# Single steps of a planned order checked by their own engines, second gate and yt tiles, and a last image in two halves

## The chip, the cores and the metric

The kernel runs on one core of a Trainium2 chip. The metric is the device time of one execution in microseconds. One further execution was taken with the hardware profiler; its trace is what the views below come from.

## The reference

Four layers on a batch of 4 images of 96 channels by 64x64 pixels (4096 tokens each), all in 32-bit floats. `gn` and `ln` are group norm and layer norm without weights.

```
x = x + ssm(gn(x))      # layer 0: 3x3 depthwise conv, 4 directional selective scans over 4096 tokens, 192 channels x 16 states
x = x + dcn(gn(x))      # layer 1: deformable 3x3 conv: offsets and mask by conv, bilinear gather of 9 taps
t = tokens(x)
t = t + fft_mix(ln(t))  # layer 2: 96->192, relu, FFT over tokens, relu of a diagonal complex map, inverse FFT, 192->96
t = t + qffn2(ln(t))    #          96->384->96, inputs and weights rounded to 8 bits (5 exponent, 2 mantissa), sums to 16
t = t + linattn(ln(t))  # layer 3: (q k^T) v for 6 heads without softmax
t = t + qffn3(ln(t))    #          as qffn2
```

The scan step is `h = exp(d*A)*h + d*u*B`, `y = C.h`, with `d = softplus(...)`. The linear attention has no softmax, so `k^T v` (96x96) is summed over all tokens first and then multiplied by `q`. A sum over the tokens is thus needed before any token's result.

## The kernel before

The program is written out by a planner on the host. Work is cut into steps: a Python generator issues some instructions and yields `cost(pe=..., dve=..., act=..., pool=...)`, its estimated time on TensorE (PE), VectorE (DVE), ScalarE (ACT) and GpSimd (POOL), or `wait(us)` for a DMA. `Clock` keeps an estimated end for each engine. The order in which the steps are drawn is the order in which each engine gets its instructions, and `in_program_order` keeps it so; each engine works through its own list in that order.

The scan is the frame. `Layer0.scan` walks over 1536 units (4 images x 4 directions x 4 stretches of 1024 tokens x 24 groups of 8 channels by 16 states). A unit is: an ACT exponential of `da` (L1003), a PE spread into `db` (L1009), a DVE multiply (`enter`, L1023), a DVE scan (`recur`, L1031), a POOL multiply (`weigh`, L1040) and PE sums into `py` (L1059). After each unit `clock.due` rises by `PACE` = 4.5 us, and two streams may fill what room is left:

- `ends`: `l0.first()` for image 0 (convolution and softplus), weights of layers 2 and 3, `l0.before(b)` for images 1 to 3 (convolution, then softplus), and then layers 2 and 3 of images 0 to 3 one after the other (`Layers23.image`). Each image waits until layer 1 has sampled it.
- `middle`: for each image `l0.behind(b)` (merge of the directions, after its scans) and `l1.image(b)` (offsets, positions, and 288 gathers, L1372, with their sums).

Where the scan can't go on, or has ended, `alone()` moves an own clock in steps of 0.5 us and offers it to the streams.

`pipe` runs several generators ("chains") of one kind side by side. It draws a chain's next step only if each engine that this step used when it last ran (`known`) is not too far ahead of the clock (`AHEAD`: 3, 3, 5, 7 us), if its tile tokens are free, and if it keeps `every` steps behind the chain before. Steps outside a `pipe`, here called single steps (group norm statistics, reciprocal roots, positions, waits for loads), are checked by `Stream.step`:

```
        if not self.piped and not (net.has_bank() and net.clock.has_room((1.0,) * 4, self.ready)):
            return False
```

So a single step needs room on all four engines, whichever it uses.

The parts that the change touches:

- `steps` (L812) makes the softplus, 48 chains an image. `ex`, `lw` and `w1` are 128x512 tiles. ACT writes `lw` (L834) and `w1` (L835), DVE combines `w1` (L838), POOL subtracts into `lw` (L840), DVE makes `rl` (L842) and frees `lw`. The pipes give `ex=3, lw=1, rl=2, du=2`.
- `Fourier.half` ends with `last` (L1573), eight chains a half: eight small products into PSUM (`yp`, L1579), an ACT copy into `yt` (L1581), one product with the weights (`o`, L1584), a DVE add to `t` (L1586). There is one `yt`.
- `centred` (L462) makes a layer norm's centred values chunk by chunk (512 tokens), gathers the variances of eight chunks in rows of one PSUM bank, and takes the reciprocal root for all at once; `normed` (L1592) spreads it again (L515) and multiplies (L1603).
- `Ffn.run` (L1633) and `LinearAttention.run` (L1699) work on all 4096 tokens: the norm first, then eight chunks of 512 (for keys and values 32 blocks of 128).
- After the scan five PSUM banks belong to the first stream and three to the other (`mm`, `has_bank`).

Of the kernel before, what the change touches and what calls it, by code (L numbers as in the profile page):

```python
# [8 lines left out]
F32 = mybir.dt.float32  # L9
# [312 lines left out]


class Stream:


    def __init__(self, net, work):
        self.net, self.work, self.ready, self.over, self.piped = net, work, 0.0, False, False
        self.held = 0

    def step(self):

        net = self.net
        net.stream = self
        if self.over or self.ready > net.clock.now():
            return False
        if not self.piped and not (net.has_bank() and net.clock.has_room((1.0,) * 4, self.ready)):
            return False
        step = next(self.work, False)
        if step is False:  # L340
            self.over = True
            return False
        self.piped = step is None or step is BLOCKED
        if isinstance(step, Step):
            self.ready = net.clock.queue(step, net.clock.now())
        return step is not BLOCKED


class Net:
# [38 lines left out]
    def mm(self, name, p=128):  # L388
        own = self.own_banks and self.stream is self.streams[0]
        return (self.own_banks if own else self.psum).tile([128, CH], F32, name=name, tag="mm")[:p]  # L390

    def has_bank(self):
        if self.own_banks:
            return self.stream.held < (5 if self.stream is self.streams[0] else 3)
        return sum(stream.held for stream in self.streams) < 3
# [65 lines left out]

    def centred(self, x, cen, dst, key, pool, bias=None):  # L462


        nc = self.nc
        var = self.mm(f"lnv{key}")
        self.hold(1)
        sqs = {}

        def chain(j):  # L470
            yield wait(new=True, takes="sq")
            cs = slice(j * CH, (j + 1) * CH)
            pc = self.mm(f"lnc{key}_{j}")
            nc.tensor.matmul(pc, lhsT=cen, rhs=x[:, cs], start=True, stop=True)  # L474
            pc = pc[:C]
            sq = sqs[j] = pool.tile([C, CH], F32, name=f"lnq{key}_{j}", tag="lnq", bufs=4)
            d, view = dst(j)
            if bias is None:
                nc.scalar.activation(sq, pc, AF.Square)
                nc.scalar.copy(d, view(pc))  # L480
            else:
                nc.scalar.activation(sq, pc, AF.Square, bias=bias)
                nc.scalar.activation(d, view(pc), AF.Identity, bias=bias)
            yield cost(pe=1.1, act=1.2, frees=f"v{j // 4}")

        def sums(r):

            yield wait(takes=f"v{r}")
            for q in range(4):
                nc.tensor.matmul(  # L490
                    var[32 * q : 32 * q + 32],
                    lhsT=self.to_row[C][:C, 1 - r : 33 - r],
                    rhs=sqs[4 * r + q],
                    start=(r == 0),
                    stop=(r == 1),
                )
            yield cost(pe=1.3, frees="sq sq sq sq")

        def chains():
            for r in range(2):  # L500
                for q in range(4):
                    yield chain(4 * r + q)
                yield sums(r)

        yield from pipe(self, chains(), 5, every=-99, sq=4, v0=-3, v1=-3)
        self.rstd = pool.tile([128, CH], F32, name=f"lns{key}", tag="lns", bufs=1)
        nw = pool.tile([128, CH], F32, name=f"lnw{key}", tag="lnw", bufs=1)
        yield from self.inv_sqrt_steps(self.rstd, var, nw, 128)
        self.hold(-1)

    def spread(self, rstd, j, n, key):
# [31 lines left out]
class Layer0:  # L543
# [54 lines left out]
    def first(self):  # L598
# [5 lines left out]
        with tc.tile_pool(name=f"l0u{b}", bufs=1) as up, tc.tile_pool(name=f"l0b{b}", bufs=1) as sm:  # L604
# [5 lines left out]
            with tc.tile_pool(name=f"l0a{b}", bufs=1) as big, tc.tile_pool(name=f"l0i{b}", bufs=1) as cp:  # L610
# [4 lines left out]
                def rows_first():  # L615
# [10 lines left out]
                    net, rows_first(), 6, every=2, lane=Layer0.conv.__code__,  # L626
                    ex=3, lw=1, rl=2, du=2, zt=1, **tokens,
                )
# [6 lines left out]

            yield from pipe(net, columns(), 5, every=2, ex=3, lw=1, rl=2, du=2)

    def before(self, b):
        net = self.net
        tc, nc, ins = net.tc, net.nc, net.ins  # L640
        with tc.tile_pool(name=f"l0u{b}", bufs=1) as up:
# [3 lines left out]
            with tc.tile_pool(name=f"l0b{b}", bufs=1) as sm:  # L645
# [12 lines left out]

                yield from pipe(self.net, chains(), 5, every=2, ex=3, lw=1, rl=2, du=2)

# [32 lines left out]
    def normed_rows(self, b, x, pad):  # L693
# [3 lines left out]
        with tc.tile_pool(name=f"l0n{b}", bufs=2) as sm:  # L697
# [17 lines left out]

            yield from net.centred(x, cen, lambda j: (rows(pad, j), as_rows), f"0_{b}", sm, bias)
            rs = net.rstd

# [93 lines left out]
    def steps(self, b, ks, j, us, dtw, sm, xdbl):  # L812
# [19 lines left out]
        nc.scalar.activation(ex, ex, AF.Exp, scale=-1.0)  # L832
        lw, w1 = tile_of("lw", 1), tile_of("w1", 1)
        nc.scalar.activation(lw, ex, AF.Ln, bias=net.one)  # L834
# [600 lines left out]
class Fourier:  # L1435
# [6 lines left out]
    def __init__(self, ctx, net):  # L1442
# [16 lines left out]
        nc.sync.dma_start(self.w2[:C], ins["w2"])  # L1459
        self.yt = wp.tile([C + 1, 8, 64], F32, name="yt")  # L1460

# [65 lines left out]
    def half(self, key, g, tv, t, pool, big):  # L1527
# [45 lines left out]
        def last(m):  # L1573
# [4 lines left out]
            for q in range(8):  # L1578
                nc.tensor.matmul(pt[:, q, :], lhsT=d[:, m + q, :], rhs=m2[:, q, :], start=True, stop=True)  # L1579
            yt = self.yt  # L1580
            nc.scalar.copy(yt[:C], pt)  # L1581
# [6 lines left out]

        yield from pipe(self.net, (last(m) for m in range(0, 64, 8)), 4, yt=1)


def normed(net, t, tl, key, pool):  # L1592

    yield from net.centred(
        t, net.cen96, lambda j: (tl[:C, j * CH : (j + 1) * CH], plain), key, pool
    )
    rs = net.rstd

    def chain(j):
        cs = slice(j * CH, (j + 1) * CH)  # L1600
        pb = net.spread(rs, 32 * (j % 4) + j // 4, C, key)
        yield cost(pe=1.2, holds=1)
        net.nc.vector.tensor_mul(tl[:C, cs], tl[:C, cs], pb)  # L1603
        yield cost(dve=0.7)

    yield from pipe(net, (chain(j) for j in range(NCH)), 3)


class Ffn:
# [22 lines left out]

    def run(self, b, t):  # L1633
        net, n = self.net, self.n
        tc, nc = net.tc, net.nc
        with tc.tile_pool(name=f"fb{n}_{b}", bufs=1) as big, tc.tile_pool(name=f"fs{n}_{b}", bufs=2) as pool:
            tl = big.tile([C, L], F32, name=f"fl{n}_{b}", tag="tl")
            yield from normed(net, t, tl, f"f{n}_{b}", pool)

# [46 lines left out]

            yield from pipe(self.net, (chunk(j) for j in range(NCH)), 4, xq=2, h16=2, h8=2, o16=2)


class LinearAttention:  # L1690
# [7 lines left out]

    def run(self, b, t):  # L1699
        net = self.net  # L1700
        tc, nc = net.tc, net.nc
        with tc.tile_pool(name=f"l3b{b}", bufs=1) as big, tc.tile_pool(name=f"l3s{b}", bufs=2) as pool:
            tl = big.tile([C + 1, L], F32, name=f"tl3{b}", tag="tl")
            nc.gpsimd.memset(tl[C:], 1.0)
            yield from normed(net, t, tl, f"3_{b}", pool)
            net.hold(1)
            pa = net.mm(f"pa{b}", C)[:, :C]

            def keys_and_values(m):
# [4 lines left out]
                yield cost(pe=0.55, act=0.4)  # L1714
                nc.tensor.matmul(pa, lhsT=kv[:, 1, :], rhs=kv[:, 0, :], start=(m == 0), stop=(m == 31))
                yield cost(pe=0.4)

            yield from pipe(self.net, (keys_and_values(m) for m in range(32)), 3)

            vk = pool.tile([C, C], F32, name=f"vk{b}", tag="vk")  # L1720
            nc.vector.tensor_mul(vk, pa, self.heads)
            net.hold(-1)
            yield cost(dve=0.3)
            p1 = net.mm(f"p1{b}", C)[:, :128]
            nc.tensor.matmul(p1, lhsT=vk, rhs=self.wff, start=True, stop=True)
            m1 = pool.tile([C, 128], F32, name=f"m1{b}", tag="m1")
            nc.scalar.copy(m1, p1)
            yield cost(pe=0.6, act=0.3)
            p2 = net.mm(f"p2{b}", C + 1)[:, :128]
            nc.tensor.matmul(p2, lhsT=self.wqT, rhs=m1, start=True, stop=True)  # L1730
            m2 = pool.tile([C + 1, 128], F32, name=f"m2{b}", tag="m2")
            nc.scalar.copy(m2, p2)
            yield cost(pe=0.6, act=0.3)

# [7 lines left out]

            yield from pipe(self.net, (chunk(j) for j in range(NCH)), 3)


class Layers23:
# [12 lines left out]
    def image(self, b):  # L1759
        net = self.net  # L1760
        while b not in self.net.sampled:
            yield BLOCKED
        with net.tc.tile_pool(name=f"t{b}", bufs=1) as tp:
            t = tp.tile([C, L], F32, name=f"t{b}", tag="t")
            net.nc.sync.dma_start(t, self.x2[b])
            yield wait(4.0)
            yield from self.fourier.run(b, t)
            yield from self.ffn2.run(b, t)
            yield from self.attn.run(b, t)
            yield from self.ffn3.run(b, t)  # L1770
            yield NOTHING
            net.nc.sync.dma_start(self.out[b], t)

# [9 lines left out]
def layers23(net, x2, out):  # L1783
# [4 lines left out]
    with ExitStack() as ctx:  # L1788
# [20 lines left out]

        streams = net.streams = [Stream(net, ends()), Stream(net, middle())]  # L1810
        clock = net.clock
# [53 lines left out]
```

## Time and profile before

| | us |
|---|---|
| median of 3 runs | 8710.01 |
| lowest, highest | 8709.18, 8720.84 |
| the profiled execution, its own time | 8725.68 |
| span of its trace | 8723.9 |
| first scan, end of the last scan | 190, 7515 |
| image 3's `t` load begins | 8261 |
| image 3's first layer norm of FFN 2 | 8541 |

All times inside the trace count from the start of its span. The busy table lists, for a stretch of the span, each engine's busy time and the number of its instructions, then the mean clock that TensorE was granted (1 is full), the share of the DMA engines and the bytes moved. The chain of waits lists start, length and engine of each piece of the work that ended last. The timeline lists start, length, engine, line and tiles, and in brackets the idle time before it with what ended it.

### The profile page before, as it was taken

To read this page: it belongs to the slowest core of one execution; us is meant where nothing else is said; L and a number is where in the kernel's file an instruction comes from. 1 tells how busy PE (TensorE), PEld (TensorE's weight loads), DVE (VectorE), ACT (ScalarE), POOL (GpSimd) and SP (SyncE) were. 2 spreads that over 40 slices of the span, in tenths; PEclk is the share of its full clock that TensorE was granted. 3 is DMA by queue.
4 is the path that set the end of the run, shared out by engine and by line. 5 is a ranking of instruction groups with operands and counts; after the bars stand their busy time and mean duration, and the time that the engine had idled before them with its cause. 6 is when DMAs were issued, how large, how long until landed. Compare 5 with 4: busy or idle time off the path is not lost.

```text
span 8723.9 us, 97214 instructions
## 1 busy us (share of the span) xinstructions
PE 6608.9 (76%) x31960; PEld 2859.5 (33%) x31960; DVE 6836.1 (78%) x5155; ACT 4925.0 (56%) x9030; POOL 5608.7 (64%) x4291
## 2 busy tenths in 40 slices
PE   6675777759767777887676788777778887789697
PEld 2211221112222332321222245422335541267383
DVE  2799889978799898778799888788988888547514
ACT  5554566636467776555577666454766665322323
POOL 0465566656579898656588887565888877347200
PEclk9765787769667777886687788776778887788788
DMA  3677678877789999766799988866879997355110
GB/s 94 160 206 186 167 199 218 211 169 193 181 217 242 242 239 231 177 169 178 194 244 239 236 222 215 188 173 165 215 207 233 229 224 170 90 153 172 56 54 13
DMA packets 773820, 1608.33 MB, mean 184 GB/s; under 512 B 264065, under 2 KB 355741, under 8 KB 771206
## 3 DMA queue, kind: packets, MB, share of 16 engines
q10 hardware_dynamic: 244224, 843.17, 38.3%
q1 hardware_dynamic: 455366, 532.37, 23.7%
q0 software_dynamic: 73728, 226.57, 9.8%
q8 instruction: 257, 4.21, 0.2%
q14 instruction: 245, 2.01, 0.1%
HBM read 1345.43 MB, written 256.29 MB: 184 GB/s over the span
## 4 chain that ended last, share of the span: by engine, by line
PE 25%; DVE 15%; DMA 7%; ACT 5%; issue 4%; SPq 1%; POOL 1%; ACTq 1%; DVEq 0%; POOLq 0%
DVE hh L1031 7%; DVE db L1023 4%; PE f L1499 3%; PE ps L1405 3%; PE py L1059 3%; PE pd L1421 2%; DMA da<-de 2%; ACT g L1384 1%; PE db L1009 1%; PE pc L752 1%; PE h L1540 1%; PE yp L1579 1%; DMA m<-in_dft 1%; ACT da L1003 1%; PE lnc L474 1%
## 5 line engine op out<-in xcount | busy, mean ns | idle before, releaser
L1040 POOL TENSOR_TENSOR hh<-hh,bc 128x1024 f32<-128x1024 f32 x1536 | 3661.0, 2386 | 377.2 <-DVE hh L1031 274.3
L1031 DVE TENSOR_TENSOR_SCAN hh<-da,st,db 128x1024 f32<-128x1024 f32 x1152 | 2700.6, 2344 | 189.4 <-PE py L1059 74.0
L1023 DVE TENSOR_TENSOR db<-db,bc 128x1024 f32<-128x1024 f32 x1536 | 1864.0, 1214 | 604.4 <-PE db L1009 602.7
L1003 ACT ACTIVATE da<-da,w_al 128x1024 f32<-128x1024 f32 x1536 | 1737.5, 1145 | 511.8 <-DMA da<-de 168.1
L1372 POOL DMA_INDIRECT g<-table,idx x1152 | 1212.7, 1053 | 373.8 <-issue 173.6
L1009 PE MATMUL db<-du,rep 24*128 24x512 bf16 x3072 | 710.0, 461 | 858.3 <-DVE hh L1031 803.5
L1059 PE MATMUL py<-hh,w_fold 128*32 128x512 f32 x6144 | 1107.7, 796 | 16.2 <-issue 11.5
L1384 ACT ACTIVATE g<-g,wt 128x96 f32<-128x96 f32 x3456 | 963.6, 364 | 136.9 <-PE py L1059 34.3
L1031 DVE TENSOR_TENSOR_SCAN hh<-da,db 128x1024 f32<-128x1024 f32 x384 | 877.3, 2285 | 84.6 <-PE py L1059 40.7
L1405 PE MATMUL ps<-w_ident,g 128*96 128x128 f32 x3744 | 736.1, 342 | 176.3 <-ACT g L1384 101.2
L1009 PEld LDWEIGHTS <-rep 24*128 24x128 bf16 x3072 | 159.6, 94 | 1963.0 <-issue 1289.7
L1038 POOL COPY st<-hh 128x1 f32<-128x1 f32 x1152 | 235.0, 204 | 741.5 <-DVE hh L1031 688.6
L1405 PEld LDWEIGHTS ps<-w_ident,g 128*96 128x96 f32 x3744 | 511.3, 149 | 548.6 <-ACT g L1384 239.0
L840 POOL TENSOR_TENSOR lw<-lw,w 128x512 f32<-128x512 f32 x192 | 243.9, 1270 | 683.7 <-DVE w L838 649.0
L752 PE MATMUL pc<-pad,wc 96*128 96x512 f32 x1152 | 579.6, 643 | 32.7 <-DMA wc<-wc_d 23.3
L871 PE MATMUL pr<-ex,w_ident 128*128 128x512 f32 x384 | 305.7, 889 | 174.7 <-DVE ex L861 81.9
L1413 ACT COPY st<-ps 96x384 f32<-96x384 f32 x384 | 178.8, 472 | 422.0 <-PE ps L1405 385.5
L752 PEld LDWEIGHTS pc<-pad,wc 96*128 96x128 f32 x1152 | 221.0, 202 | 361.5 <-issue 314.3
L829 PE MATMUL pd<-xd,w_dtw 103*64 103x512 f32 (+1 forms) x512 | 275.7, 821 | 52.7 <-DVE rl L842 18.8
L1421 PE MATMUL pd<-st,wdc 96*128 96x256 f32 x1152 | 308.9, 419 | 1.3 <-DVE d L1548 1.1
L1508 ACT COPY d<-f 128x512 f32<-128x512 f32 x192 | 111.9, 583 | 301.8 <-PE f L1499 297.1
L1059 PEld LDWEIGHTS py<-hh,w_fold 128*32 128x32 f32 x6144 | 158.5, 125 | 355.2 <-issue 282.9
(252 smaller groups left out, 8915.4 us busy)
## 6 DMA issues: line engine op xcount, KB each, us to landing
da<-de ACTq DMA_DIRECT2D x1536, 512.0 KB
du<-du SPq DMA_DIRECT2D x1536, 96.0 KB
bc<-bcd SPq DMA_DIRECT2D x128, 512.0 KB
y<-yb SPq DMA_DIRECT2D x384, 128.0 KB
de<-rl SPq DMA_DIRECT2D x128, 256.0 KB
m<-in_dft SPq DMA_DIRECT2D x128, 256.0 KB
ad<-y ACTq DMA_DIRECT2D x192, 128.0 KB
table<-pix SPq DMA_DIRECT2D x256, 96.0 KB
```

The costliest lines, as they stand in the source:

```text
L752: nc.tensor.matmul(pp, lhsT=wc[:, q, g * 128 : (g + 1) * 128], rhs=pad[:, r0 + dy : r0 + dy + NR, dx : dx + W], start=(q == 0), stop=(q == 8),
L871: nc.tensor.matmul(pr, lhsT=net.ident, rhs=ex, start=True, stop=False)
L1003: self.net.nc.scalar.activation(u.da, u.da, AF.Exp, scale=self.al[:, a : a + 1])
L1009: self.net.nc.tensor.matmul(db[:, h, :], lhsT=self.rep[64 * u.q + 32 * h : 64 * u.q + 32 * h + 24], rhs=u.du[64 * u.q + 32 * h : 64 * u.q ...
L1023: self.net.nc.vector.tensor_mul(u.db, u.db, u.bc[:, 0, :])
L1031: nc.vector.tensor_tensor_scan(u.along(u.hh), u.along(u.da), u.along(u.db), first, ALU.mult, ALU.add)
L1040: self.net.nc.gpsimd.tensor_mul(u.hh, u.hh, u.bc[:, 1, :])
L1059: nc.tensor.matmul(py[p0 : p0 + 32], lhsT=self.fold[:, u.i, :], rhs=hc[:, h * CH : (h + 1) * CH], start=u.sums["add"] is None and u.i == 0 ...
L1372: nc.gpsimd.indirect_dma_start(out=g[:, k, :], out_offset=None, in_=self.tables[b % 2], in_offset=bass.IndirectOffsetOnAxis(ap=idx[:, n : ...
L1384: nc.scalar.activation(pixel, pixel, AF.Identity, scale=wt[:, n, c : c + 1])
L1405: nc.tensor.matmul(pt[:, k, :], lhsT=g[:, k, c * C : (c + 1) * C], rhs=net.ident, is_transpose=True, start=(c == 0), stop=(c == corners - 1),)
L1421: nc.tensor.matmul(po, lhsT=wdc[:, k, :], rhs=st[:, k, :], start=(k == 0), stop=(k == 8))
```

## The change

A single step is now checked by the work it had when the program last stood at the same place (code object and line of the innermost generator); only at an unknown place are all four engines asked for room.

```
+def place(steps):
+    while steps.gi_yieldfrom is not None and hasattr(steps.gi_yieldfrom, "gi_code"):
+        steps = steps.gi_yieldfrom
+    return steps.gi_code, steps.gi_frame.f_lineno

 class Stream:
-    def __init__(self, net, work):
+    def __init__(self, net, work, own=False):
...
-        self.held = 0
+        self.held, self.own = 0, own
     def step(self):
...
-        if not self.piped and not (net.has_bank() and net.clock.has_room((1.0,) * 4, self.ready)):
+        here = place(self.work) if self.work.gi_frame else None
+        work = net.known.get(here, (1.0,) * 4)
+        if not self.piped and not (net.has_bank() and net.clock.has_room(work, self.ready)):
             return False
...
         if isinstance(step, Step):
+            if not self.piped:
+                net.known[here] = step.work
             self.ready = net.clock.queue(step, net.clock.now())
```

The gate tiles `lw` and `w1`, and `yt`, get a second buffer, and the pipes a second token:

```
-                    ex=3, lw=1, rl=2, du=2, zt=1, **tokens,
+                    ex=3, lw=2, rl=2, du=2, zt=1, **tokens,
...
-        lw, w1 = tile_of("lw", 1), tile_of("w1", 1)
+        lw, w1 = tile_of("lw", 2), tile_of("w1", 2)
...
-        self.yt = wp.tile([C + 1, 8, 64], F32, name="yt")
+        self.yt = wp.tile([C + 1, 2, 8, 64], F32, name="yt")
...
-            yt = self.yt
+            yt = self.yt[:, m // 8 % 2]
...
-        yield from pipe(self.net, (last(m) for m in range(0, 64, 8)), 4, yt=1)
+        yield from pipe(self.net, (last(m) for m in range(0, 64, 8)), 4, yt=2)
```

The last image's FFN 2, attention and FFN 3 run as two streams, each with half of the tokens (`groups=(0,)` or `(1,)`, four chunks of 512) and tile pools on its own side. Half 0 has the five own banks, half 1 the three shared ones. `centred`, `normed`, `Ffn.run` and `LinearAttention.run` take `groups`; each half makes its own norm with its own reciprocal root over a whole 128x512 tile. In the attention each half sums its own `vk`; half 0 waits for both, adds them and makes `m2`, half 1 waits for `m2`, and both wait for each other at the end. Each half stores its own 2048 tokens.

```
+            if len(groups) == 1:
+                while len(shared) < 2:
+                    yield BLOCKED
+                if groups[0] == 0:
+                    nc.vector.tensor_add(vk, vk, shared[1])
+                    yield cost(dve=0.3)
+            if groups[0] == 0:
                 p1 = net.mm(f"p1{b}", C)[:, :128]
...
+                m2 = shared["m2"] = pool.tile([C + 1, 128], F32, name=f"m2{b}", tag="m2")
...
+            while "m2" not in shared:
+                yield BLOCKED
+            m2 = shared["m2"]
...
+            shared[f"over{groups[0]}"] = True
+            while len(groups) == 1 and not ("over0" in shared and "over1" in shared):
+                yield BLOCKED
```

```
             yield from self.fourier.run(b, t)
-            yield from self.ffn2.run(b, t)
...
+            shared = {}
+            def half(r, side):
+                yield from self.ffn2.run(b, t, (r,), side)
+                yield from self.attn.run(b, t, (r,), side, shared)
+                yield from self.ffn3.run(b, t, (r,), side)
+                cs = slice(L // 2 * r, L // 2 * (r + 1))
+                net.nc.sync.dma_start(self.out[b][:, cs], t[:, cs])
+                yield NOTHING
+
+            halves = [Stream(net, half(0, "left"), own=True), Stream(net, half(1, "right"))]
+            net.streams += halves
+            while not all(h.over for h in halves):
+                yield BLOCKED
```

Images 0 to 2 run as before, over all tokens.

## The prediction

> **What bounds the kernel now.** I read the page's totals first, then the busy table by stage, then the chain of waits at the end, then two single tiles.
>
> ```profile
> PE 6608.9 (76%) x31960; PEld 2859.5 (33%) x31960; DVE 6836.1 (78%) x5155; ACT 4925.0 (56%) x9030; POOL 5608.7 (64%) x4291
> ```
>
> No engine is full over the whole span. The busy table (PE, PEld, DVE, ACT, POOL, then clock, DMA share, GB/s) says why:
>
> ```profile
> 2400.00:3500.00 1100.00, 814.98 (x3384) 318.14 (x3382) 1000.74 (x667) 790.79 (x1754) 955.26 (x742) 0.74 0.90 234
> 3500.00:4300.00 800.00, 616.79 (x1928) 188.67 (x1927) 596.72 (x416) 427.37 (x602) 448.66 (x342) 0.74 0.70 175
> 5000.00:5400.00 400.00, 344.84 (x2513) 209.04 (x2514) 326.01 (x216) 269.11 (x658) 333.60 (x266) 0.85 0.91 226
> 7707.00:8145.00 438.00, 376.73 (x3147) 297.92 (x3146) 311.83 (x411) 127.71 (x255) 337.76 (x289) 0.86 0.57 167
> 8262.00:8541.00 279.00, 243.98 (x2641) 211.20 (x2642) 46.35 (x63) 63.17 (x115) 0.00 (x0) 0.89 0.18 52
> 8541.00:8600.00 59.00, 39.25 (x96) 12.89 (x96) 34.24 (x65) 26.07 (x50) 3.83 (x1) 0.79 0.00 0
> 8600.00:8660.00 60.00, 52.40 (x199) 28.29 (x198) 14.39 (x22) 21.20 (x54) 0.00 (x0) 0.95 0.00 1
> 8660.00:8724.00 64.00, 36.67 (x95) 11.62 (x93) 32.16 (x68) 26.41 (x51) 0.00 (x0) 0.77 0.08 25
> ```
>
> Up to 7515 the scans run: 1536 of them, 7515-190 = 7325 us, 4.8 us each, against 1.21 (multiply, L1023) + 2.34 (scan, L1031) = 3.55 us of VectorE. With softplus and sampling beside it (2400 to 3500) VectorE is 91% busy and bounds. With convolution and `behind` beside it (3500 to 4300) it is 75% busy, the rate is 5.7 us a unit, and the waits of VectorE name TensorE: 603 us in all for `db`. After 7515 come 1209 us of tail. Image 2's layers 2 and 3 end in it at 8254, and only then does image 3's `t` load start, though image 3's last gather was issued at 8141. The last rows are image 3 alone: nothing runs beside it, and FFN 2 and FFN 3 keep TensorE 67% and 57% busy.
>
> The chain of waits over one Fourier half's last stage, and the softplus tiles while sampling runs (timeline):
>
> ```profile
> 8523.54 1.35 PE yp L1579 x16
> 8524.96 0.59 ACT yt L1581
> 8525.60 1.13 PE o L1584 x2
> 8526.72 1.35 PE yp L1579 x16
> ```
>
> ```profile
> 2709.62 0.72 ACT L834 ACTIVATE lw<-ex,one 128x512 f32<-128x512 f32 x1 [0.17 <-DVE rl L842]
> 2713.89 1.98 DVE L838 SCALAR_TENSOR_TENSOR w<-w,ex 128x512 f32<-128x512 f32 x1
> 2725.72 1.27 POOL L840 TENSOR_TENSOR lw<-lw,w 128x512 f32<-128x512 f32 x1
> 2737.18 0.68 DVE L842 SCALAR_TENSOR_TENSOR rl<-pd,lw 128x512 f32<-128x512 f32 x1
> ```
>
> One `yt` makes TensorE, ScalarE and TensorE take turns every 3.18 us. One `lw` is held for 28 us here, 12 of them behind other work on POOL, and the next chain can't start until it is free.
>
> **1. Last image as two streams.** From 8540.8 (first `lncf`) to 8723.9 it takes 183 us, 8 of them the output store. Dense TensorE work, by the warm pace of the chain: a layernorm 16 x 0.43 (centre) + 3.7 (sums) + 16 x 0.43 (spread) = 17.5, three of them 52; an FFN chunk 6 x 0.43 = 2.6, sixteen of them 41; keys and values 4 passes x 0.18 x 32 blocks = 23; the rest 8. Sum 125. VectorE has 80.8 busy in these rows. Added: each half does its own rsqrt over 128x512 (ScalarE 0.70+0.64+0.64, VectorE 0.76+0.44+0.70), so three more of these, 6 us on each engine; one `vk` product and one add (0.3 each); one more store issue. TensorE's other half hides them; were it idle, they would cost 12. Two barriers in attention remain (half 0 needs both `vk`, half 1 needs `m2`, both wait for each other at the end); I charge 3 us each, plus 12 for the last FFN chunk's run through four engines and 8 for the store: 125+6+12+8 = 151, a saving of 32. Here the granted clock matters. The rows show 0.79, 0.95 and 0.77 for the three stages against 0.89 in the Fourier stage, and the first `lnbf` passes are 0.85 us apart, later ones 0.43. [...] I take 28, since only the VectorE-bound chunks remain thin; ends 10 and 40.
>
> **2. `yt` doubled.** With two tiles the next `yp` is queued before `o`, so the 0.7 us that `o` waits for `yt` (the waits show 12.6 us over 19 times, 0.66 each) lies under TensorE work. Period 1.5+1.13 = 2.63 instead of 3.18: 0.55 x 8 x 2 = 9 us for image 3, on the end path. For images 0 to 2 it shortens their stream only. VectorE's 1.26 us add still fits the period. I take 9; ends 5 and 11.
>
> **3. `lw` and `w1` doubled.** Not an instruction more. The planner keeps each chain three steps behind the one before (`every=2`), so the second tile frees a chain from one step, the wait for `rl` after POOL's subtract. In the sampling stages 48 chains take 1050 us per image (`lw` at 2269 to 3320 and 3925 to 4980), 22 us each; in image 1's stage, with POOL free, about 540 us, 11 each. I expect 22 to fall to about 16: 48 x 6 = 290 us earlier for image 2, the same again for image 3. No trace row shows two in flight, so the ends are 0 and 48 x 11 = 530 per image. This is time of the stream `ends`, not of the kernel: those chains have about 2.7 us of VectorE each, which only moves to earlier units of a VectorE-bound scan.
>
> **4. Single steps by their own work.** No instruction more; they are queued up to one unit (4.5 us planned) sooner, some 40 of them per image and stream with dependencies of their own. Taken at 1 to 2 us each, 40 to 80 us per image of stream time. Past them move the DMA issues on SP that sit in them (`base`, `xr`, `t`, weights), unchanged in number. What is queued behind such a step on VectorE is the next scan, and behind that `db` on TensorE and the weigh on POOL. A step fed by a DMA that is late then stops all of them; the second rival prices this.
>
> **What steps 3 and 4 buy.** `ends` gets to image 0's layers 2 and 3 up to 600 us earlier than 4991 (gate: image 0 sampled, about 3600). Images 1 and 2 are gated by sampling (image 1 about 5440, image 2 about 7160), so image 2 starts near 7160 instead of 7617 and is no longer last. The tail is then bound by the stream `middle`: gathers from 7707, 288 of them. They took 434 us beside the Fourier stages; at 0.98 + 0.30 issue each they need 369. I take half of that 65, 30, and the whole wait between image 3's last store (about 8160) and its `t` load (8261), 100. Against it, some 124 us of image 2's work moves in front of 7515; at the tail's 25% VectorE share it is 31 us of VectorE, in a scan phase with 1014 us of VectorE idle: between 0 and 36, I take 20.
>
> **Sum, in the profiled execution's own frame:** 8723.9 - 28 - 9 - 100 - 30 + 20 = 8577 of span, 147 less. The profiled execution took 8725.7, 16 above the median of the three runs, 8710; so 8710 - 147 = 8563, and I say 8560.
>
> **The rivals.** (a) The streams stay in their order and image 2's end stays last. Then only what is local counts: 28 + 9 for image 3, 9 for image 2's `yt`, and some 20 for single steps in the tail: 66, 8644. For it: image 1 ends at 7610 and its gates leave slack at each image; against it: 600 us of head start. (b) The scan phase itself gets shorter: image 3's convolution moves from 3500 to 3950, where it meets `behind(1)` and TensorE makes VectorE wait (86 us in 300), into the sampling stage before. If the 800 us at 5.7 us a unit run at 4.8, that is 125 us more: 8435. For it: 91% against 75% VectorE. Against it: TensorE's 74% to 86% has to find room elsewhere, which is 5000 to 5400's rate (4.6). (c) Slower: head-of-line waits on VectorE. In the scan phase it stood 18.3 us once for `base` alone, and about 100 us for DMAs in all, sampling's `xr` included. Some 20 such steps are now queued up to one unit sooner, while the DMA behind them lands no sooner: 20 x 4.5 = 90 us; with the POOL backlog of two softplus chains ahead of the weigh, another 40. It decides once it exceeds (a)'s 66: +64, 8774 at worst, 8750 likely. (d) That the change does little because the planner's order is set elsewhere (`every=2`, the gates) is (a) without its single steps, 8664.
>
> **How the numbers follow.** Forecast (8490 to 8610 by itself) 0.56; (a) and (d) 0.25; (b) 0.11; (c) 0.08. What a measurement here tells from no change is about 0.2%, 17 us. (a) and (d) lie beyond it; between them and (c) a small overlap gives "same" 0.03, and (c) keeps 0.06. The range goes from (b), 8435, to the upper side of (a), 8680; it leaves out most of (c) and the far side of (b).
>
> **What would show it.** Right: image 3's `t` load starts within 20 us of its last sampled store, and image 2's output store lies before it; image 0's `t` load comes before 4700; `lw` stages of images 2 and 3 take under 850 us; `o` no longer waits for `yt`; from the last Fourier add to the end about 155 us with a granted clock over 0.85; the last scan between 7430 and 7600. Wrong: the last scan ends after 7650 with longer VectorE waits on DMAs (rival c), or image 2's store is still the step before image 3's load (rival a).

## The result, and the profile after

| | before | after |
|---|---|---|
| median, us | 8715.0 (8709.2 to 8720.8) | 8608.1 (8600.5 to 8613.7) |
| ratio, with its 95% interval | | 0.9877 (0.986 to 0.9894) |
| span of the trace | 8723.9 | 8598.7 |

The change saves 107 us; the forecast was 150 us, 8560. The trace of after belongs to an execution of 8600.5 us, so the two traces differ by 125.2 us. That difference falls apart like this:

| piece | before | after | difference | forecast |
|---|---|---|---|---|
| start of the span to image 3's last sampled store | 8154.5 | 8171.2 | +16.6 | -10 (+20 and -30) |
| from there to image 3's `t` load | 107.0 | 1.8 | -105.2 | -100 |
| Fourier layer of image 3, load to last add | 279.2 | 249.8 | -29.5 | -9 |
| last add to the end (FFN 2, attention, FFN 3, store) | 183.1 | 175.9 | -7.2 | -28 |
| sum, before rounding | | | -125.2 | -147 |

The engines' totals of the page of after show little of it: the work is the same, and what moved is where it lies.

```profile
PE 6553.4 (76%) x31960; PEld 2840.7 (33%) x31960; DVE 6817.9 (79%) x5118; ACT 4945.4 (58%) x9071; POOL 5626.7 (65%) x4308
```

**The order at the end.** First SP's timeline of before, then of after. Each line is a transfer's start, the issue's length, and what goes where; `x<-xo` is a store of a sampled image, `t<-x` the load of image 3 into layer 2.

```profile
8154.52 0.30 SPq L1428 DMA_DIRECT2D x<-xo  x1
8254.23 0.32 SPq L1772 DMA_DIRECT2D out<-t  x1
8261.49 0.30 SPq L1765 DMA_DIRECT2D t<-x  x1
```

```profile
8171.17 0.30 SPq L1439 DMA_DIRECT2D x<-xo  x1
8172.96 0.30 SPq L1805 DMA_DIRECT2D t<-x  x1
```

Before, the load stood behind image 2's output store, 107 us after the last store of its own data. After, it follows its own data at once; image 2's output store lies at 8030. This one line is 105 of the 125 us.

**The stages.** The busy table of before and then of after, cut at the last scan and at the last sampled store (PE, PEld, DVE, ACT, POOL, each with its count; then clock, DMA share, GB/s). The first pair of rows is before's.

```profile
190.00:7510.00 7320.00, 5515.02 (x24622) 2148.38 (x24621) 6243.21 (x4239) 4455.18 (x8156) 5231.75 (x3964) 0.76 0.80 203
7510.00:8155.00 645.00, 521.64 (x3779) 362.79 (x3780) 385.28 (x555) 199.35 (x394) 360.26 (x311) 0.84 0.48 135
```

```profile
190.00:7550.00 7360.00, 5615.11 (x25947) 2243.60 (x25947) 6272.92 (x4294) 4530.84 (x8307) 5241.03 (x3978) 0.77 0.80 203
7550.00:8171.00 621.00, 455.20 (x2725) 295.88 (x2722) 374.56 (x534) 177.38 (x363) 366.61 (x311) 0.80 0.47 131
...
8173.00:8423.00 250.00, 227.88 (x2641) 199.47 (x2642) 45.56 (x63) 63.26 (x115) 0.00 (x0) 0.96 0.20 58
8423.00:8599.00 176.00, 133.00 (x388) 53.97 (x387) 88.71 (x165) 78.80 (x164) 7.45 (x2) 0.79 0.03 9
```

Some 1,300 of the streams' matmuls (24622 against 25947) now run beside the scan instead of behind it. The scan phase is 40 us longer, the stretch behind it 24 us shorter, and nearly all of these 24 lie between the last scan and image 3's first gather (7510 to 7707 before, 7550 to 7724 after). The Fourier row has TensorE 91% busy at a clock of 0.96 (before 87% at 0.89). The last row has the forecast's second stream in it, and still TensorE is busy for 133 of 176 us, at 0.79. The two halves don't end together either: half 0 issues its output store at 8578.7 and half 1 at 8593.4, and in the 15 us between them half 1 is alone:

```profile
8579.00:8594.00 15.00, 7.96 (x17) 1.77 (x16) 10.88 (x25) 5.89 (x11) 0.00 (x0) 0.57 0.17 52
```

**`yt`.** The chain of waits at the end of the Fourier layer of after. `yp` and `o` of two chunks at a time follow each other on TensorE with nothing between:

```profile
8402.89 2.93 PE yp L1590 x32
8405.82 1.80 PE o L1595 x4
8407.62 2.69 PE yp L1590 x32
8410.31 1.85 PE o L1595 x4
```

The second pair takes 4.54 us for two chunks, 2.27 each, which is the pace of both halves of the layer. The prediction set 2.63 against 3.18.

**Softplus.** The timeline of after near the place that the prediction showed of before:

```profile
2709.38 1.28 POOL L851 TENSOR_TENSOR lw<-lw,w 128x512 f32<-128x512 f32 x1
2715.20 0.72 ACT L845 ACTIVATE lw<-ex,one 128x512 f32<-128x512 f32 x1
...
2719.84 0.68 DVE L853 SCALAR_TENSOR_TENSOR rl<-pd,lw 128x512 f32<-128x512 f32 x1
```

ScalarE writes the next `lw` (2715) before VectorE has read the last one (2719.8): two are in flight. A chain is not as much faster as was hoped. From first `lw` to last `rl`, image 2's 48 chains took 952 us instead of 1087 and image 3's 926 instead of 1019, 19.6 us a chain where 16 was forecast.

### The profile page after: what moved, and what is told of

Read it like the earlier page. It is cut to its first block, busy times and chain, and to the rows that moved or that the text cites. A ratio compares the mean times of both kernels' runs of the same rounds, so it can differ in the third digit from the quotient of the medians.

```text
span 8598.7 us, 97186 instructions
## 1 busy us (share of the span) xinstructions
PE 6553.4 (76%) x31960; PEld 2840.7 (33%) x31960; DVE 6817.9 (79%) x5118; ACT 4945.4 (58%) x9071; POOL 5626.7 (65%) x4308
## 4 chain that ended last, share of the span: by engine, by line
PE 27%; DVE 14%; DMA 7%; ACT 7%; issue 4%; POOL 2%; ACTq 1%; SPq 1%; DVEq 0%; POOLq 0%
DVE hh L1042 7%; DVE db L1034 3%; PE ps L1416 3%; PE f L1510 3%; PE py L1070 3%; DMA da<-de 2%; PE pd L1432 2%; ACT g L1395 2%; PE db L1020 2%; ACT da L1014 1%; PE h L1551 1%; PE yp L1590 1%; PE zp L1576 1%; POOL hh L1051 1%; PE py L1065 1%
## 5 line engine op out<-in xcount | busy, mean ns | idle before, releaser
L1416 PE MATMUL ps<-w_ident,g 128*96 128x128 f32 x3744 | 688.8, 329 | 222.8 <-issue 90.6
```

Of the source, the lines that this page charges most:

```text
L1416: nc.tensor.matmul(pt[:, k, :], lhsT=g[:, k, c * C : (c + 1) * C], rhs=net.ident, is_transpose=True, start=(c == 0), stop=(c == corners - 1),)
```

## The experiments

The same program took a little longer or shorter from one batch to the next: before's median was 8715 above, 8786 in the first batch below, 8782 in the second and 8697 in the third. So times are compared within a batch, and all ratios are to before of the same batch. After itself had 0.9877 above and 0.9821 in the second batch, so differences of about half a per cent between batches tell nothing. Each trace is one execution, and can be up to some 30 us faster or slower than its kernel's median.

### First batch: after with one part undone (before 8786)

**u_half**, the last image in one stream:

```
-            if b < B - 1:
+            if b < B:
```

> The changed kernel with the last image's FFN 2, attention and FFN 3 in one stream again. Theory (lockstep): the two halves enter every stage together, both norms on TensorE, then both FFNs on VectorE, so they saved only what the trace shows from the last Fourier add to the end, 183.2 - 175.9 = 7 us; expected 8608 + 7 = 8615, ratio to the kernel before 0.988 to 0.990. Rival (the prediction's step 1): 28 us, 8636, ratio 0.991.

8659 us, ratio 0.9849 (0.9814 to 0.9884). That is below both ratios that were expected, which lay closer together than the scatter between batches, so the trace has to decide. Its busy table from the `t` load on:

```profile
8235.00:8483.00 248.00, 224.89 (x2640) 197.94 (x2640) 45.53 (x63) 63.27 (x115) 0.00 (x0) 0.97 0.20 59
8483.00:8666.00 183.00, 131.49 (x388) 53.71 (x388) 80.85 (x155) 73.98 (x155) 3.83 (x1) 0.82 0.03 9
```

With one stream the last stretch is 183 us long, just as before the change, and TensorE's busy time in it is the same 131 to 133 us. Four traces with one stream (before, u_half, a_lw, a_step) have 183.1 to 186.8; six with two streams and nothing else changed there (after, after_again, u_yt, u_lw, u_step, u_step_2) have 173.1 to 176.3. The second stream is worth 7 to 14 us. The rest of what u_half's trace is longer by had arisen before that: its load lies at 8235, after's at 8173, in an order of instructions that is the same up to there.

**u_yt**, one `yt`:

```
-            yt = self.yt[:, m // 8 % 2]
+            yt = self.yt[:, 0]
...
-        yield from pipe(self.net, (last(m) for m in range(0, 64, 8)), 4, yt=2)
+        yield from pipe(self.net, (last(m) for m in range(0, 64, 8)), 4, yt=1)
```

> The changed kernel with one yt tile and one token again. Theory (clock): the alternation of TensorE and ScalarE costs 0.55 us a chunk and, in a half in which the granted clock falls, doubles the period to 5.3 us as in the first half of image 3 before; the last stages of image 3 took 41.7 + 27.0 us before and 19.0 + 20.5 after, so 29 us come back if one half is slow again: 8637. Rival (the prediction's step 2): only the 0.55 us, 9 us, 8617. The trace decides by the period of yp in the two halves: 5.3 and 3.2 or 3.2 and 3.2.

8643 us, ratio 0.982 (0.979 to 0.9849). In its trace image 3's Fourier layer took 281.3 us, against 247 to 251 in the traces with two tiles. Its chain of waits, first in one half of the layer, then in the other:

```profile
8338.69 1.35 PE yp L1590 x16
...
8340.75 1.12 PE o L1595 x2
8341.87 1.35 PE yp L1590 x16
```

```profile
8453.98 2.52 PE yp L1590 x16
...
8457.21 2.08 PE o L1595 x2
8459.29 2.52 PE yp L1590 x16
```

The same instructions have a period of 3.18 us in the first and 5.31 in the second. In before it is the first half that is slow. Its chain again:

```profile
8388.88 2.52 PE yp L1579 x16
...
8392.12 2.08 PE o L1584 x2
8394.19 2.52 PE yp L1579 x16
```

The prediction had read the other half alone. The busy table of before over the eight chunks of the slow half and then of the fast one has the granted clock (third figure from the end) that goes with it:

```profile
8385.00:8424.00 39.00, 33.25 (x143) 24.40 (x143) 8.76 (x7) 4.65 (x8) 0.00 (x0) 0.53 0.16 47
8513.00:8541.00 28.00, 20.25 (x148) 14.66 (x146) 10.11 (x8) 5.23 (x9) 0.00 (x0) 1.00 0.12 39
```

In u_yt it is 0.94 over 8211 to 8350, and 0.84 over 8350 to 8492, in which the slow chunks lie. So the clock theory holds, and the rival, 3.18 in both halves, does not. Two tiles give 2.27 in both halves: (3.18 - 2.27) x 8 + (5.31 - 2.27) x 8 = 32 us, near the 29.5 and 31.5 of the traces. The median doesn't show this: u_yt's ratio is that of after_again below (0.9821). But the profiled execution was the slowest of its six (8620 to 8668), and the ratios' intervals are wider than the 30 us in question.

**u_lw**, one gate tile (`lw=1` in the three pipes):

```
-        lw, w1 = tile_of("lw", 2), tile_of("w1", 2)
+        lw, w1 = tile_of("lw", 1), tile_of("w1", 1)
```

> The changed kernel with one lw and one w1 tile and lw=1 again; single steps by their own work stay. Theory (second gate tile carries the head start): image 0's t load goes back from 4579 to about 4950, image 2's output store is again the last thing before image 3's load, and some 80 of the 88 us come back: 8690. Rival (single steps carry it): image 0's load stays before 4750 and the time rises by under 20 us.

8726 us, ratio 0.9927 (0.9901 to 0.9954), by far the dearest part to lose. The writes of `lw` in image 3's stage, first of u_lw, then of after:

```profile
L845 ACT ACTIVATE lw<-ex,one x48: 721/722/724, 3805.6 to 4883.6; 128x512 f32<-128x512 f32 x48
```

```profile
L845 ACT ACTIVATE lw<-ex,one x48: 721/722/728, 3637.2 to 4530.8; 128x512 f32<-128x512 f32 x48
```

1078 us for the 48 writes, against 894. So image 0's `t` load comes at 4909 and image 2 is last again: its store is issued at 8284.8, the load of image 3 at 8292.1, 74 us after the last sampled store at 8218.4. The wait that the change removed is back.

**u_step**, all four engines asked for room again:

```
-        work = net.known.get(here, (1.0,) * 4)
+        work = (1.0,) * 4
```

> The changed kernel with room on all four engines asked for at every single step again; tiles and halves stay changed. Theory (second gate tile carries the head start): image 0's t load stays before 4750, image 3's load still follows its own last sampled store, and the time rises by 10 to 30 us for single steps in the chain: 8620 to 8640. Rival (single steps carry it): image 0's load goes to about 4900 and the time rises by 60 us or more. Third possibility: earlier single steps cost more by waiting for DMAs on VectorE than they bring, and the time falls.

8598 us, ratio 0.978 (0.975 to 0.9809). Undoing this part loses nothing; the time lies on the side of the third possibility. In its trace the last scan starts at 7460, after's at 7548, and image 3's load comes at 8159, although image 0's load is 110 us later than in after (4688 against 4579). The next batch has both kernels.

### Second batch: the own-work check, and the two streams (before 8782)

**after_again** is after, unchanged, and **u_step_2** is u_step, unchanged, each to stand beside the other.

> The changed kernel itself, as the yardstick of this batch: the kernel before took 8786 in the last batch and 8715 in the one that gave the result, so the undone parts are to be read against the changed kernel of the same batch. Expected ratio to before 0.978 to 0.988.

> Room on all four engines asked for at every single step, the rest changed, once more, beside the changed kernel. If single steps by their own work cost (their first trace had its last scan end at 7462, against 7550 in the changed kernel's trace and 7586 in the one-stream kernel's, whose order up to there is the same), this is faster than the changed kernel by 30 to 90 us. If they bring 10 to 30 us, as the prediction had it, it is slower by that; if they do nothing, within 15.

after_again 8621 us, ratio 0.9821 (0.9794 to 0.9847); u_step_2 8580 us, ratio 0.9788 (0.9759 to 0.9817). Without the own-work check the kernel is 41 us faster by the medians; the two intervals overlap. The two traces lie further apart, 77 us, since the one of after_again is the slowest of its five executions and the one of u_step_2 the fastest of its five. They show where the time differs. Busy tables, first after_again, then u_step_2, each up to the last scan and from there to the last sampled store:

```profile
190.00:7564.00 7374.00, 5622.65 (x25950) 2253.84 (x25949) 6270.82 (x4294) 4530.76 (x8307) 5241.99 (x3978) 0.77 0.79 203
7564.00:8211.00 647.00, 463.88 (x2721) 300.18 (x2719) 372.32 (x534) 177.46 (x362) 353.66 (x311) 0.79 0.44 126
```

```profile
190.00:7436.00 7246.00, 5470.96 (x24914) 2154.20 (x24916) 6276.10 (x4282) 4514.89 (x8268) 5239.41 (x3978) 0.78 0.80 206
7436.00:8132.00 696.00, 547.52 (x3756) 381.56 (x3748) 380.26 (x546) 196.79 (x401) 359.68 (x311) 0.81 0.43 123
```

VectorE has the same work in both scan phases (6271 and 6276 us). TensorE has 152 us and 1,036 matmuls more in the one of after_again, and the scan phase is 128 us longer; the part behind is 49 us shorter. But most of the added matmuls don't lie where the time is lost. Cut at the scan's unit 1440 of 1536 (after_again, then u_step_2):

```profile
190.00:7081.00 6891.00, 5260.01 (x23788) 2087.62 (x23787) 5891.00 (x4033) 4299.20 (x7919) 4930.97 (x3751) 0.77 0.80 205
190.00:6964.00 6774.00, 5114.65 (x23547) 2033.99 (x23546) 5882.18 (x4007) 4271.46 (x7842) 4917.04 (x3744) 0.78 0.81 208
```

By then 117 of the 128 us are lost with only 241 matmuls more, while TensorE is already busy 145 us longer. The other 800 or so matmuls fall into the last 96 units and cost 11 us. What VectorE waits for in the scan phase (us in total, times, longest), after_again and then u_step_2:

```profile
DVE db L1034 <- PE db L1020: 573.1, 269, 30.6
DVE hh L1042 <- PE py L1070: 95.7, 90, 5.2
```

```profile
DVE db L1034 <- PE db L1020: 496.2, 250, 17.7
DVE hh L1042 <- PE py L1070: 83.2, 78, 6.4
```

89 us more of waiting for TensorE's `db` and `py`. The rows that name a DMA sum to 77 us in the one and 80 in the other, so late transfers at the head of VectorE's queue (the third rival) are not the price. Why TensorE comes later with the scan's `db` in that order stays open. In all six traces that have gate tiles and the own-work check during the scan (after, after_again, u_half, u_yt, stag, stag_ones), the last scan starts between 7537 and 7584 and image 3's load comes between 8173 and 8235; in the five with gate tiles and without that check during the scan (u_step, u_step_2, a_lw, best1, late_ones), between 7434 and 7474, and 8116 and 8160.

**stag**: half 1 enters each FFN norm only after half 0 has left its own, so that the two are not in the same stage at the same time.

```
-    def run(self, b, t, groups=(0, 1), side="left"):
+    def run(self, b, t, groups=(0, 1), side="left", behind=None):
...
+            while behind is not None and behind not in net.passed:
+                yield BLOCKED
...
+            net.passed.add((n, groups))
```

> The changed kernel with half 1 held back: it enters the norm of FFN 2, and of FFN 3, only when half 0 has left that norm. No instruction more or less. Theory (lockstep): norm of one half beside FFN of the other, so the stretch from the last Fourier add to the end falls from 176 to about 140 us (14 for the first norm, 16 and 16 for the FFN chunks on VectorE, 24 for half 1's second norm and its keys and values, 3 for the merge, 5, 12, 16 and 16, and 5 for the store, with some loss), 20 to 40 us less than the changed kernel. Rival (engines are full there anyway, or the barriers take it): under 8 us.

8638 us, ratio 0.9842 (0.9816 to 0.9868); the last stretch took 184.0 us, 7.6 more than in after_again. Holding half 1 back by one norm thus doesn't make the halves fit beside each other; another spacing was not tried.

**stag_ones**: as stag, and the row of ones below the attention's `tl` is copied by ScalarE from the ones that `yt` has in its last row. The reason lies in VectorE's timeline of after:

```profile
8450.17 3.59 POOL L1726 MEMSET tl<- 1x4096 f32 x1 [287.14 <-DVE xqf L1664]
8450.54 3.88 DVE L1678 TENSOR_SCALAR h16f<-h16f,bias 128x512 f16<-128x512 f16 x3
...
8455.81 0.86 DVE L1678 TENSOR_SCALAR h16f<-h16f,bias 128x512 f16<-128x512 f16 x3
```

The group of three takes 3.88 us while POOL's memset runs and 0.86 without it. Each half has a memset, so it happens twice in after (3.88 at 8450.5 and 4.21 at 8469.1) and happened once in before.

```
-            nc.gpsimd.memset(tl[C:], 1.0)
+            if ones is None:
+                nc.gpsimd.memset(tl[C:], 1.0)
+            else:
+                for r in groups:
+                    for q in range(2):
+                        c0 = L // 2 * r + 1024 * q
+                        nc.scalar.copy(tl[C:, c0 : c0 + 1024], ones)
```

> As the one before, and the row of ones under the attention's normed tokens of the last image is copied by ScalarE (two copies of 1x1024 a half) instead of being set by POOL. In the trace of the changed kernel each of the two POOL memsets (3.6 and 3.9 us) lies over a VectorE group of 16-bit adds that takes 3.9 and 4.2 us instead of 0.87. Theory (the memset holds VectorE up): the slow groups are gone and the time falls by 3 to 6 us more. Rival: the groups are slow for another reason and stay.

8635 us, ratio 0.9836 (0.981 to 0.9862). VectorE's timeline of stag_ones at the same place:

```profile
8466.48 0.87 DVE L1682 TENSOR_SCALAR h16f<-h16f,bias 128x512 f16<-128x512 f16 x3
8467.38 0.96 DVE L1690 CAST h8f<-h16f 128x1536 fp8e5<-128x1536 f16 x1
8468.26 0.87 DVE L1682 TENSOR_SCALAR h16f<-h16f,bias 128x512 f16<-128x512 f16 x3
```

No long one is left in the stretch; stag, with the memsets, has two of them, 4.20 us in its timeline and 3.72 in its chain of waits. The stretch is 180.8 instead of 184.0 us; the medians differ by 2, less than they scatter.

### Third batch: before with one part, and the better version (before 8697)

**a_lw**: before with the second gate tile alone; **a_step**: before with the own-work check alone.

```
-                    ex=3, lw=1, rl=2, du=2, zt=1, **tokens,
+                    ex=3, lw=2, rl=2, du=2, zt=1, **tokens,
...
-        lw, w1 = tile_of("lw", 1), tile_of("w1", 1)
+        lw, w1 = tile_of("lw", 2), tile_of("w1", 2)
```

> The kernel before with two lw and two w1 tiles and lw=2, nothing else. Theory (the second gate tile alone makes the head start, and the end is bound by what comes last after the scan): image 0's t load at about 4690 instead of 4991, image 3's load 70 to 100 us earlier, ratio to before 0.988 to 0.992. Rival (the head start needs the single steps too): ratio above 0.996.

8648 us, ratio 0.9945 (0.9928 to 0.9961), between what the theory and the rival expected; the trace, which has the theory's head start, is of the fastest of its 22 executions (8618). Image 0's load moves from 4991 to 4678 by this part alone, image 2's store comes 1 us after the last sampled store, and image 3's load follows at 8160, 8.5 us after the last sampled store. With one `yt`, both halves of its Fourier layer had the period of 3.18 us, and the layer took 269.6 us.

```
-        if not self.piped and not (net.has_bank() and net.clock.has_room((1.0,) * 4, self.ready)):
+        here = place(self.work) if self.work.gi_frame else None
+        work = net.known.get(here, (1.0,) * 4)
+        if not self.piped and not (net.has_bank() and net.clock.has_room(work, self.ready)):
...
+            if not self.piped:
+                net.known[here] = step.work
```

> The kernel before with single steps checked by their own last work, nothing else. Theory (it moves work of the stream ends into the scan phase, and the scan pays for it at TensorE): image 0's load some 80 us earlier, last scan no earlier than before, time within 0.5% of before, ratio 0.995 to 1.001. Rival (the prediction's step 4: 40 to 80 us of stream time an image, on the end path while image 2 is last): 60 us or more, ratio below 0.993.

8650 us, ratio 0.9933 (0.991 to 0.9957). The ratio misses the theory's range; alone, the check is a gain too. In its trace the scan doesn't pay for it: the last scan starts at 7468, 40 us earlier than in before. Image 0's load is 59 us earlier (4932), and image 2's store, still the step before image 3's load, 75 us (8179.5). Both parts buy the same thing, that image 2 ends sooner, and once it is no longer last, more of it is worth nothing.

**best1**: u_step with the ones of stag_ones. **late_ones**: the same, but with the own-work check from the end of the scan on:

```
-        work = (1.0,) * 4
+        work = net.known.get(here, (1.0,) * 4) if net.own_banks else (1.0,) * 4
```

> The changed kernel with room on all four engines asked for at every single step again, and the last image's row of ones copied by ScalarE instead of set by POOL. It joins the two edits that were better than the changed kernel: ratio 0.978 as the first had it, less 3 to 6 us, so about 0.9775, 8584 where before takes 8782. If the two don't add up, 0.979 to 0.982.

> As the one before, but single steps are checked by their own work once the scan has ended. Theory: during the scan this check costs (the last scan came some 100 us later with it), after the scan it costs nothing and image 2's end, which is again the last thing before image 3's load there (stores at 8122 and 8147, loads at 8133 and 8159), comes a little earlier: 10 to 20 us below the one before, ratio about 0.976. Rival (after the scan the check is without effect because TensorE is taken): the same within 8 us.

best1 8553 us, ratio 0.9823 (0.9797 to 0.9849); late_ones 8538 us, ratio 0.9801 (0.9775 to 0.9827). Both have a last stretch of 172.0 us, the shortest of all, and image 3's load at 8116 to 8118. So the check after the scan did not bring that load the 10 to 20 us forward that were expected: in both traces image 2's store already lies before the last sampled store (8105 and 8116, 8088 and 8115). Late_ones has the lowest median of the batch, but its interval overlaps that of best1, and after was not run beside them. That they beat after is thus read from the second batch (u_step_2 against after_again) and from these stretches of the traces, not from one comparison of their own.

## Why the prediction was right, and where not

**The main step held.** Image 3's wait for image 2's end was to save 100 us and saved 105.2. The load starts 1.8 us after its last sampled store (forecast: within 20), image 2's store lies before it, image 0's load comes before 4700, and `o` no longer waits for `yt`. u_lw, which puts the old wait back, and a_lw, in which it is down to 8.5 us, show that the gate tile is what decides it. The first rival, in which image 2 stays last, is what u_lw and a_step are.

**Image 3's `yt`: 9 forecast, 29.5 measured.** The failed term is the old period of 3.18. It came from one half's chain and was used for both; the other half ran at 5.31, at a clock of 0.53. The lines for this were in the trace of before, one half earlier. The new period (2.27, forecast 2.63) was mis-sized too, since TensorE takes two chunks in a row. Not every kernel with one `yt` has a slow half: a_lw has none, and its layer took 269.6 us, so some 10 of the 29.5 us hang on a slow half that isn't always there.

**Two streams: 28 forecast (10 to 40), 7.2 measured**, 7 to 14 over the traces. The sum of dense work, 125 us, was nearly right: TensorE was busy for 133. What failed is that the rest would be hidden: 43 of the 176 us are beside TensorE's work, where the forecast left 26 to 30. No run shows the 28 us, nor the clock over 0.85 that went with them; both were the author's estimate. The runs show 7 to 14 us, and no higher clock with two streams: over the last stretch it was 0.84 in before and 0.82 in u_half, with one stream, and 0.79 in after, with two and TensorE 76% busy. In its three parts (FFN 2, attention, FFN 3) it went from 0.79, 0.95 and 0.77 to 0.80, 0.88 and 0.80 (8423 to 8482, to 8537, to 8579). At most 3 of the missing us are the second memset. By stages, FFN 2 and attention went from 118.5 to 114.4, FFN 3 from 56.5 to 56.3, and the store from 8.1 to 5.3. In FFN 3, 15 of the 56 us are half 1 alone, with TensorE busy for 8 of them at a clock of 0.57. Why it falls behind stays open: it has three PSUM banks against the five of half 0 and is offered its steps second, and neither was tried otherwise. In the 42 us before that no engine was over 77% busy, and holding one half back a norm made it longer.

**The gate tile: 16 us a chain forecast, 19.6 measured**, stages of 952 and 926 us where "under 850" was to be seen: 134 and 94 us gained instead of 290 twice. The row for it was the prediction's own: VectorE was 91% busy in the sampling stage, and over the 952 us it is still 88% (836.9). A chain that no longer waits for its tile waits for VectorE: over image 2's 48 chains, the mean time from ScalarE's `w1` to VectorE's combining of it rose from 2.8 to 5.6 us. The chain that the prediction read was not typical either: it held `lw` for 28 us, where the mean of these 48 in before is 18.5. The head start of image 0's load, 413 us (313 with the gate tile alone, 59 with the check alone), was enough, and more than enough.

**Gathers: 30 forecast, nothing measured.** From the first to the last they took 434 us in both traces. The group of POOL in after, from 7700 to 8180 (busy time, mean ns of one; idle time before it, and what ended it):

```profile
L1383 POOL DMA_INDIRECT g<-table,idx x288 | 340.2, 1181 | 163.3 <-DVE wt L1363 71.2 <-issue 62.9 <-DVE g L1403 8.2
```

340 us busy and 63 of issue are 403 of the 434 us: POOL does little but issue them, and no faster stream takes work from it. The prediction had used 0.98 us, the median, where the mean of these 288 in before is 1.16.

**Longer scans: +20 forecast, +41 between the two traces.** The prediction priced the moved work at 31 us of VectorE and took 20. VectorE's work in the scan phase rose by 30 us (6243 to 6273 in the rows above), and its waits for `db` did not rise (before, then after):

```profile
DVE db L1023 <- PE db L1009: 602.7, 262, 26.0
DVE db L1034 <- PE db L1020: 584.4, 278, 29.1
```

So the price was of the right kind; the 11 us that are left are less than the scatter, as the last scan starts at 7548, 7562 and 7584 in after, after_again and u_half, whose order is the same up to there. What the sum left to rival (b) is that the scan phase gets shorter with the gate tile alone: in the five traces without the check during the scan, the last scan starts 33 to 74 us earlier than in before, and in a_lw VectorE waits for TensorE for 683 us of the scan phase, against 776 in before. The check takes this back; by which work of TensorE stays open.

**The single steps** were charged as a part of the head start, with late DMAs as their risk. Alone that holds (a_step, 0.9933). Beside the gate tile they are a loss in the traces: the scan phase is longer, with longer waits for TensorE and not for DMAs. That they cost the 41 us between the two medians is likely, not certain, as the intervals overlap.

**The sum.** Errors of 21 us (streams) and 27 (everything up to the last sampled store) on one side and of 20 (`yt`) and 5 (the load) on the other leave 22 of the 147. That the two terms of the last image, both outside their own ranges, nearly cancel is luck. The other 26 us between 8560 and 8608 are no part of the change: 16 were taken off because before's profiled execution was that much above its median, after's profiled execution was 8 below its own, and 3 were rounded off. Three small readings were off without deciding anything: the last scan ends at 7510, not 7515; VectorE is idle for 1082 us up to 7515 (7325 - 6243), not 1014; and image 3's `lw` stage starts at 3962, not 3925.

## What to carry to other kernels

A head start in an ordered program is worth only what the one late piece behind it needs: find that piece and give it that much. An order of steps can also make the main loop longer or shorter with the same instructions: here two kinds of order ended the scan at least 63 us apart, so look at the main loop's end after each part of such a change. Before a period is multiplied by a count, look at it in every part of the count, since the same instructions can run at two speeds (periods of 3.18 and 5.31 us here). Where two streams are to fill each other's gaps, an engine's idle time is not yet room for the other: here a quarter of TensorE's time stayed idle with two, and one stream ended 15 us before the other.

## What the runs showed of the hardware

**Two speeds of one pattern.** With one `yt`, TensorE works 2.47 of every 3.18 us (1.35 and 1.12, 78%) or 4.60 of every 5.31 us (2.52 and 2.08, 87%). The slow one set in with the second of a half's eight chunks (8388.9 in before, 8454.0 in u_yt) and lasted to the last. In before the granted clock was 0.53 over the chunks with 5.31 us (8385 to 8424) and 1.00 over those with 3.18 us (8513 to 8541); the same `yp` and `o` took 1.87 and 1.86 times as long, and 1.00 / 0.53 is 1.89. The pauses are 0.7 us long in both, and the busier of the two is the slow one; what sets off the longer period can't be read from these traces. With two tiles no pause is left: over image 3's layer `o` waits for `yt` 16 times in before, 11.5 us in all, and not once in after, whose clock over the last chunks (8400 to 8423) is 1.00.

**A memset of one partition holds VectorE.** POOL's 1x4096 memset (3.5 to 3.9 us) stretches a group of three 16-bit VectorE operations (128x512 each) from 0.87 to 3.88 and 4.21 us. The two groups of after end 0.66 and 0.15 us after the memset beside them does (8454.42 against 8453.76, 8473.35 against 8473.20), and with ScalarE making the row (stag_ones) a group takes 0.87 again. By what the memset holds VectorE does not show in the traces.
